# Last softmax blocks of two steps, weights divided first, products in PSUM, and step 0's weights straight from the gathered rows

## The chip, the cores and the metric

The kernel runs on one core of a Trainium2 chip. The metric is the device time of one execution in microseconds (us), as the median of repeated executions. One full pass is about 2.08 ms. The profiles are of single executions.

SBUF and PSUM are the two memories beside the engines (matmuls write to PSUM, which is handed out in banks), HBM is the large one outside. In profile lines PE is TensorE and PEld its weight loads, DVE is VectorE, ACT ScalarE, POOL GpSimd, and SP SyncE, which issues transfers (DMA). L952 is line 952 of that run's kernel, x8 a count of instructions, and the clock is the share of TensorE's full clock that was granted.

Two kinds of chip come up in this study. In three sets of runs the kernel before takes 2081 to 2082 us; in one set, all on one chip, it takes 2095.6 us (median of 45 runs). I call that kind of chip slow, and never compare a time of one kind with a time of the other. (This is my word: the record puts all timed runs but one in the fast state, and that one is unknown.) Points of profiles are compared across the two kinds in places; the chip column of the table below shows where.

## The reference

A recommender with a history of T = 100 steps, 128 features, 1024 samples. Cut to what matters:

```python
# phase 1: a GRU over the history, and an attention score for each of its states
_, gru_seq = scan(gru_step, h0, swapaxes(item_historical_embedding, 0, 1))
keys  = swapaxes(gru_seq, 0, 1)                       # (sample, step, feature)
score = mlp(concat([keys, q, keys - q, q * keys]), relu)
attn  = softmax(where(mask == 1, score, -inf), axis=1)
pooled = einsum('bt,btd->bd', attn, keys)
att_seq = pooled.T[:T]                                # feature t of pooled is step t's weight
# phase 2: a second recurrence (AUGRU), whose update gate is scaled by that weight
def augru_step(h, (x_t, a_t)):
    r = sigmoid(concat([h, x_t]) @ Wr.T + br)
    u = sigmoid(concat([h, x_t]) @ Wu.T + bu)
    h_hat = tanh(concat([h * r, x_t]) @ Wh.T + bh)
    u = a_t[:, None] * u
    return (1 - u) * h + u * h_hat
```

Phase 2 needs the *finished* pooled vector before its first step, so between the two loops there is a serial passage: finish the softmax, finish the pooling, bring the pooled rows into the order of phase 2 (sorted by length), start.

## The kernel before

The samples are in two halves of 512. The softmax is an online one in blocks of steps. Pooling is a multiplication of keys and weights and an addition; GpSimd does it during the loop, and after the loop GpSimd takes half 0 and VectorE takes half 1. The pooled rows are written to HBM, gathered in sorted order by indirect DMA, transposed on TensorE into a table of weights (one row for each step), written to HBM once more, and read back broadcast over the partitions, one row for a step. The parts that the change touches, cut (`...` marks cuts):

```python
ENDS = (*range(8, 89, 8), 92, 96, T)          # ends of the softmax blocks

def pool(self, count, eng):                   # VectorE or GpSimd
    ...
    w = e[:, self.ks, n].unsqueeze(2).to_broadcast(acc.shape)
    ...
    d = wp.tile([P, KH, R], F32, tag=tag, name="kw")      # SBUF
    eng.tensor_mul(d, k, w)
    eng.tensor_add(acc, acc, d)

# the end of phase 1
    ...
    for half in reversed(halves):             # mask * 1/den, then the last pooling
        nc.vector.tensor_mul(att[half.i], used, 1/den)
    for half, eng in zip(reversed(halves), (nc.vector, nc.gpsimd)):
        half.pool(T, eng)
        nc.vector.tensor_mul(att[half.i], att[half.i], pooled[:, half.ks, :])
        for p in range(P // R):
            nc.sync.dma_start(out=to[p], in_=att[half.i][p * R : (p + 1) * R])

# phase 2
def sort_weights(i, r, gates):                # r: the gathered rows of half i
    p = bank("pw") if i else pa.tile(...)
    for g in range(GH):
        nc.tensor.transpose(p[:, ts(g, P)], r[:, g, :], ident)
    rows_t = wp.tile([P, HB], F32, name="att_t", bufs=2)
    nc.vector.tensor_copy(rows_t, p)
    nc.sync.dma_start(out=att_d[i], in_=rows_t[:T, :])
    first = pa.tile([P, HB], F32, tag="a", name="first")
    nc.tensor.matmul(first, lhsT=ident[:, 0:1].to_broadcast([P, P]), rhs=rows_t, ...)
    u, h = gates
    nc.vector.tensor_mul(first, first, u)
    nc.vector.tensor_mul(h3[i], first, h)     # the state after step 0
    for t in (1, 2):
        load_att(t, i)                        # read the table's row t, broadcast
```

The pool `pa` has a single PSUM bank; `bank()` rotates through the other seven. The order of phase 2's start on TensorE, which is program order, is: gates of step 0, then the six input products of the gates of step 1 (`open_gates`), `sort_weights(0)`, the recurrent products of step 1 for half 0, `sort_weights(1)`, the transposes of the keys of step 2, the candidate product of step 1 (`ph<-r,wh`), and so on through the loop.

## Time and profile before

| kernel before | |
|---|---|
| time, median of 3 (range) | 2082.06 us (2079.63 to 2083.44) |
| span of the profiled execution | 2094.8 us |
| TensorE / VectorE busy | 97% / 84% |
| last GRU operation of phase 1 starts | 1414.67 us |
| first write of pooled rows to HBM | 1456.9 us |
| first recurrent product of phase 2 | 1474.6 us |

The page, the table by stretch and the waits are quoted in the prediction. One more view is needed for what follows: TensorE's own timeline where phase 2 starts. Each line has the start, the busy time of the group, engine, line, operation, output and inputs, shape, count, and in brackets how long the engine stood idle before it and what ended that.

```profile
1460.54 2.08 PE L967 MATMUL pr<-k,wr 128*128 128x512 f32 x2 [7.89 <-ACT k L954]
...
1469.74 0.33 PE L919 MATMUL pw<-ident,att_r 128*128 128x128 f32 x1 [0.98 <-DMA att_r<-pooled_d,idx]
...
1481.92 0.66 PE L953 MATMUL pk<-ident,rows 128*128 128x128 f32 x4 [1.52 <-DVE first L932]
1482.41 1.02 PE L971 MATMUL ph<-r,wh 128*128 128x512 f32 x2
```

TensorE has opened the gates of step 1 (from 1460.54 on) and then waits for the last gathered row of half 0, which lands at 1469.7. The last line, the candidate product of step 1, is the point from which the loop runs; call it the **restart**. The key transposes and the gates of step 0 were done long before, from 1441.3 to 1452.7, while VectorE still pooled.

### The profile page before, as it was taken

Reading aid. Unit: us, or ns where it says so; the run is one execution under the profiler, and the core shown is the slowest. Engines: PE = TensorE matmul, PEld = TensorE weight load, DVE = VectorE, ACT = ScalarE, POOL = GpSimd, SP = SyncE. Lnnn points to the kernel's source line nnn. Section 1 sums busy time; section 2 is a strip of 40 time slices with the busy share of each in tenths; the row PEclk is TensorE's granted clock in tenths of the full one; section 3 lists DMA queues with packets and bytes.
Section 4 is the critical chain, followed back from the end, with each engine's and each line's share of the span. In section 5 each row is a group of like instructions: output and inputs, shape, how many; then the busy total and the mean of one; then the engine's idle time right before and its main releaser. Section 6 shows DMA issues by size and latency. Waiting matters only on the chain. (4 is left out here: it accounts for less than half of the span.)

```text
span 2094.8 us, 26717 instructions
## 1 busy us (share of the span) xinstructions
PE 2042.1 (97%) x8292; PEld 977.6 (47%) x8292; DVE 1758.4 (84%) x3025; ACT 826.1 (39%) x1508; POOL 1302.3 (62%) x1301
## 2 busy tenths in 40 slices
PE   8999999999999999999999999996799999999998
PEld 3343333333333333333333333333344556678887
DVE  6888999999989988989898888998467777888786
ACT  3334343433434343433343333432343444445454
POOL 0234939579796959595969586796645444444332
PEclk9999999999999999999999999998999999999999
DMA  4643233333234434333433332222533333333331
GB/s 119 113 93 102 87 102 110 98 105 87 85 95 111 115 104 114 110 109 95 137 107 98 91 95 79 82 87 69 158 95 111 96 93 96 98 99 96 78 73 34
DMA packets 254611, 205.60 MB, mean 98 GB/s; under 512 B 75846, under 2 KB 216874, under 8 KB 254458
## 3 DMA queue, kind: packets, MB, share of 16 engines
q1 hardware_dynamic: 242138, 171.36, 29.5%
q0 software_dynamic: 12320, 32.44, 5.6%
q8 instruction: 67, 1.10, 0.2%
q14 instruction: 86, 0.70, 0.1%
HBM read 147.68 MB, written 54.40 MB: 96 GB/s over the span
## 5 line engine op out<-in xcount | busy, mean ns | idle before, releaser
L490 PE MATMUL ps<-x,wih 128*128 128x512 f32 x1200 | 592.7, 603 | 4.1 <-DMA x<-in_hist_x 4.1
L490 PE MATMUL ps<-hn,whh 128*128 128x512 f32 x1188 | 574.4, 592 | 0.0
L490 PEld LDWEIGHTS ps<-x,wih 128*128 128x128 f32 x1200 | 220.9, 190 | 327.7 <-issue 254.4
L490 PEld LDWEIGHTS ps<-hn,whh 128*128 128x128 f32 x1188 | 225.7, 190 | 284.1 <-issue 276.3
L476 POOL TENSOR_TENSOR xm<-x,m 128x512 f32<-128x512 f32 x200 | 246.5, 1233 | 127.3 <-DMA m<-mask_d 127.0
L521 ACT ACTIVATE ps<-ps,bih 128x512 f32<-128x512 f32 x200 | 132.4, 662 | 470.3 <-DVE ps L520 470.3
L502 ACT ACTIVATE r<-ps,brz 128x512 f32<-128x512 f32 x200 | 137.4, 687 | 394.4 <-PE ps L490 393.6
L477 POOL TENSOR_TENSOR hist<-hist,xm 128x512 f32<-128x512 f32 x200 | 265.8, 1329 | 15.7
L580 POOL TENSOR_TENSOR pooled<-pooled,kw 128x512 f32<-128x512 f32 x190 | 255.4, 1344 | 14.9
L579 POOL TENSOR_TENSOR kw<-kt,e 128x512 f32<-128x512 f32 x190 | 219.8, 1157 | 64.1 <-DVE e L735 64.0
L159 POOL DMA_INDIRECT rows<-keys_d,idx_k x208 | 202.2, 972 | 84.0 <-POOL rows L158 49.8
L559 DVE TENSOR_TENSOR kq<-hn,item 128x512 f32<-128x512 f32 x200 | 228.0, 1179 | 0.0
L638 PE MATMUL pm<-hn,wk 128*32 128x512 f32 x1200 | 213.3, 598 | 5.3 <-DVE f L672 3.6
L638 PE MATMUL pm<-kq,wkq 128*32 128x512 f32 x1200 | 210.9, 594 | 0.0
L979 ACT ACTIVATE c<-ph,bh 128x96 f32<-128x96 f32 (+42 forms) x198 | 96.7, 488 | 270.9 <-PE ph L971 228.2
L638 PE MATMUL pm<-mv,w 128*32 128x512 f32 (+1 forms) x808 | 198.2, 602 | 2.2 <-ACT mv L677 1.7
L995 DVE TENSOR_TENSOR pu<-pu,c 128x96 f32<-128x96 f32 (+42 forms) x197 | 88.8, 451 | 112.3 <-ACT c L979 90.6
L158 POOL COPY rows<-rest 128x1 f32<-128x1 f32 x208 | 39.1, 188 | 223.0 <-DVE rest L1005 218.7
L672 DVE TENSOR_TENSOR f<-pm,q 128x512 f32<-128x512 f32 x200 | 128.4, 684 | 55.8 <-PE pm L638 55.8
L525 DVE TENSOR_TENSOR d<-hn,ps 128x512 f32<-128x512 f32 x198 | 136.1, 687 | 34.9 <-ACT ps L521 32.6
L526 DVE TENSOR_TENSOR d<-ps,d 128x512 f32<-128x512 f32 x200 | 138.4, 692 | 23.8 <-ACT ps L522 7.1
L520 DVE TENSOR_TENSOR ps<-ps,u 128x512 f32<-128x512 f32 x200 | 140.0, 700 | 21.6 <-PE ps L490 0.5
(158 smaller groups left out, 3019.7 us busy)
## 6 DMA issues: line engine op xcount, KB each, us to landing
x<-in_hist_x SPq DMA_DIRECT2D x212, 256.0 KB
keys_d<-kt SPq DMA_DIRECT2D x46, 1024.0 KB
m<-mask_d SPq DMA_DIRECT2D x200, 128.0 KB
keys_d<-kt SPq DMA_DIRECT2D x64, 64.0 KB
rows<-keys_d,idx_k POOLq DMA_INDIRECT x208
s_b<-mv SPq DMA_DIRECT2D x200, 8.0 KB
mask_i<-in_mask SPq DMA_DIRECT2D x8, 200.0 KB
at<-att_d SPq DMA_DIRECT2D x32, 48.0 KB
```

Of the source, the lines that this page charges most:

```text
L159: nc.gpsimd.indirect_dma_start(out=r[:, k, :], out_offset=None, in_=keys_d[q], in_offset=bass.IndirectOffsetOnAxis(ap=idx_k[:, k, i : i + ...
L476: nc.gpsimd.tensor_mul(d, x, m)
L477: nc.gpsimd.tensor_add(acc, acc, d)
L490: nc.tensor.matmul(p, lhsT=w[:, g, :], rhs=v, start=(j == 0), stop=(j == len(parts) - 1),)
L502: nc.scalar.activation(r, pr, AF.Sigmoid, bias=brz[:, 0:1])
L520: nc.vector.tensor_add(pi, pi, u)
L525: nc.vector.tensor_sub(d, h, pi)
L526: nc.vector.tensor_mul(d, pz, d)
L559: nc.vector.tensor_mul(kq, h, item[:, self.cols])
L579: eng.tensor_mul(d, k, w)
L580: eng.tensor_add(acc, acc, d)
L638: nc.tensor.matmul(p[i][s, :], lhsT=w[:, s], rhs=v, start=start, stop=stop)
```

## The change

The intent is to shorten the passage. (a) The last block of four steps becomes two of two, so that GpSimd and VectorE can pool the first pair while the second is still being scored. (b) The weights are divided by their sum before pooling, so the two 512-column products of mask and reciprocal go. (c) The weights, and the products that VectorE makes in the tail, lie in PSUM, so that its operations don't read two operands from SBUF while GpSimd reads there too. (d) Half 1's last score rectification goes from VectorE to ScalarE. (e) Step 0's weights are taken from the gathered rows by four small broadcast matmuls, ahead of the transposes and the copy. (f) Converted keys get a pool of their own. For (c) six PSUM banks are set aside until the last pooling (`banks` below), and the products of the features (`pf`), which fill TensorE meanwhile, go to two of them in a changed order. The diff is cut (`...`), and long lines are shortened:

```diff
-ENDS = (*range(8, 89, 8), 92, 96, T)
+ENDS = (*range(8, 89, 8), 92, 96, 98, T)
@@ pool
+                    psum = eng is nc.vector and e[1] is not None
+                    w = e[psum][:, self.ks, n].unsqueeze(2).to_broadcast(acc.shape)
...
+                        if psum:
+                            d = blocked(banks["kw"])
+                        else:
+                            d = wp.tile([P, KH, R], F32, tag="kw", name="kw")
@@ scores
-                elif half.i:
-                    nc.vector.tensor_scalar(to, of, bias, 0.0, ALU.add, ALU.max)
@@ sums of the last block
                     nc.vector.reciprocal(den, den)
+                    nc.vector.tensor_mul(e[:, :, :rows], e[:, :, :rows], den ...)
+                if both[1] is not None:
+                    nc.vector.tensor_copy(both[0][:, :, :rows], e[:, :, :rows])
@@ end of phase 1
+        names = [ps.tile([P, HB], F32, tag="g", name="last") for _ in range(6)]
+        banks.update(e=names[:2], kw=names[2], pt=names[3], f=names[4:])
... (stages, pooling of block A by both engines, then of block B)
-        for half in reversed(halves):
-            nc.vector.tensor_mul(att[half.i], used, 1/den)
+        for half in halves:
+            nc.vector.tensor_mul(t, later["used"][:, half.ks, :], pooled[:, half.ks, :])
@@ sort_weights
+            first = pa.tile([P, HB], F32, tag="a", name="first")
+            for g in range(GH):
+                nc.tensor.matmul(first[:, ts(g, P)],
+                    lhsT=r[:, g, 0:1].to_broadcast([P, P]), rhs=ident, ...)
+            u, h = gates
+            nc.vector.tensor_mul(first, first, u)
+            nc.vector.tensor_mul(h3[i], first, h)
+            p = pa.tile([P, HB], F32, tag="a", name="pw") if i else bank("pw")
             ... transposes, copy, write of the table (as before)
-            first = ... (broadcast matmul from rows_t, the two products)
@@ load_key
-            k = wp.tile([P, HB], F32, name="k3", bufs=4)
+            k = qp.tile([P, HB], F32, name="k3")
```

More of the change, by code (lines that the diff above doesn't have):

```diff
@@ L568, in pool @@
                     acc = pooled[:, self.ks, :]
-                    w = e[:, self.ks, n].unsqueeze(2).to_broadcast(acc.shape)
+                    psum = eng is nc.vector and e[1] is not None
+                    w = e[psum][:, self.ks, n].unsqueeze(2).to_broadcast(acc.shape)
                     if t is None:
@@ L576, in pool @@
                     else:
-                        tag = "d" if eng is nc.vector else "kw"
-                        d = wp.tile([P, KH, R], F32, tag=tag, name="kw")
+                        if psum:
+                            d = blocked(banks["kw"])
+                        else:
+                            d = wp.tile([P, KH, R], F32, tag="kw", name="kw")
                         eng.tensor_mul(d, k, w)
@@ L607, in features @@
                 )
-                p = ps.tile([P, M0], F32, tag="g", name="pf")
+                p = banks["f"][g % 2][:, :M0]
                 for c, v in enumerate(comb):
@@ L624, in features, with blocked @@
                 yield
+        def blocked(t):
+            return t.rearrange("p (k r) -> p k r", r=R)
         halves = [Half(i) for i in range(NH)]
         left = {}
+        banks = {}
         def attend(t):
@@ L706, in softmax @@
             e = sp.tile([P, NK, 2 * G + 1], F32, name="e", bufs=3)
+            both = e, None
+            if banks:
+                b = banks["e"].pop()
+                both = e, b[:, : NK * (G + 1)].rearrange("p (k n) -> p k n", n=G + 1)
+                e = both[1]
+                top_n, den_n = (b[:, NK * m : NK * (m + 1)] for m in range(G + 1, G + 3))
             top = sp.tile([P, NK], F32, name="top", bufs=3)
             den = sp.tile([P, NK], F32, name="den", bufs=3)
-            soft.update(j=j + 1, top=top, den=den)
+            if both[1] is None:
+                top_n, den_n = top, den
+            soft.update(j=j + 1, top=top, den=den, e=both)
             def scores(i):
                 ks = ts(i, KH)
-                pt = pa.tile([P, KH, R], F32, tag="a", name="pt")
+                if banks:
+                    pt = blocked(banks["pt"])
+                else:
+                    pt = pa.tile([P, KH, R], F32, tag="a", name="pt")
                 nc.vector.transpose(
@@ L721, in tops @@
                 scores(1)
-                nc.vector.tensor_reduce(top, e[:, :, :n], AX.X, ALU.max)
+                nc.vector.tensor_reduce(top_n, e[:, :, :n], AX.X, ALU.max)
                 if j:
-                    nc.vector.tensor_max(top, top, top_old)
-                    nc.vector.tensor_sub(e[:, :, n], top_old, top)
+                    nc.vector.tensor_max(top, top_n, top_old)
+                    nc.vector.tensor_sub(e[:, :, n], top_old, top_n)
+                    if both[1] is not None:
+                        nc.vector.tensor_scalar_min(e[:, :, n], e[:, :, n], 0.0)
                 nc.vector.tensor_sub(
@@ L735, in sums @@
                 nc.vector.tensor_mul(e[:, :, :n], e[:, :, :n], on)
-                nc.vector.tensor_reduce(den, e[:, :, :n], AX.X, ALU.add)
+                nc.vector.tensor_reduce(den_n, e[:, :, :n], AX.X, ALU.add)
                 if j:
@@ L739, in sums @@
                     nc.vector.tensor_mul(old, den_old, e[:, :, n])
-                    nc.vector.tensor_add(den, den, old)
+                    nc.vector.tensor_add(den, den_n, old)
                 if last:
                     nc.vector.reciprocal(den, den)
+                    nc.vector.tensor_mul(
+                        e[:, :, :rows],
+                        e[:, :, :rows],
+                        den.unsqueeze(2).to_broadcast([P, NK, rows]),
+                    )
+                if both[1] is not None:
+                    nc.vector.tensor_copy(both[0][:, :, :rows], e[:, :, :rows])
                 for half in halves:
                     if j:
-                        half.todo.append((e, n, None))
-                    half.todo += [(e, t - b0, t) for t in range(b0, b1)]
+                        half.todo.append((both, n, None))
+                    half.todo += [(both, t - b0, t) for t in range(b0, b1)]
             soft["stages"] += [lambda: scores(0), tops, sums]
@@ L839, in gru_phase @@
         stage()
+        e, _ = soft["e"]
+        copy = banks["e"][0][:, : NK * (G + 1)].rearrange("p (k n) -> p k n", n=G + 1)
+        nc.vector.tensor_copy(copy, e[:, :, : G + 1])
+        for half in halves:
+            half.todo = [((w[0], copy if w[0] is e else None), n, t) for w, n, t in half.todo]
         halves[0].pool(T, nc.gpsimd)
@@ L847, in gru_phase @@
         some(features[1:2])
-        halves[1].pool(1, nc.vector)
+        halves[1].pool(2, nc.vector)
+        stage()
         take(T)
@@ L851, in gru_phase @@
         attend(T + 1)
-        some(features[2:6])
-        halves[1].pool(1, nc.vector)
+        some(features[2:4])
+        stage()
         take(T + 1)
+        exponents()
+        some(features[2:4])
         halves[1].pool(T, nc.vector)
-        some(features[2:6])
+        some(features[4:6])
+        stage()
+        halves[0].pool(T, nc.gpsimd)
         stage(2)
-        some(features[6:])
+        some(features[4:6])
         exponents()
         some(features[6:])
+        some(features[6:])
         stage()
-        att = [
-            t.rearrange("p (k r) -> p k r", r=R)
-            for t in s_bs[NH * (soft["j"] % 2) : NH * (soft["j"] % 2) + NH]
-        ]
-        for half in reversed(halves):
-            nc.vector.tensor_mul(
-                att[half.i],
-                later["used"][:, half.ks, :],
-                soft["den"][:, half.ks].unsqueeze(2).to_broadcast([P, KH, R]),
-            )
-        for half, eng in zip(reversed(halves), (nc.vector, nc.gpsimd)):
-            half.pool(T, eng)
-            nc.vector.tensor_mul(att[half.i], att[half.i], pooled[:, half.ks, :])
+        halves[0].pool(T, nc.gpsimd)
+        halves[1].pool(T, nc.vector)
+        for half in halves:
+            t = blocked(s_bs[NH * (soft["j"] % 2) + half.i])
+            nc.vector.tensor_mul(t, later["used"][:, half.ks, :], pooled[:, half.ks, :])
             to = pooled_d[half.cols, :].rearrange("(k r) (p c) -> p r k c", r=R, c=R)
             for p in range(P // R):
-                nc.sync.dma_start(out=to[p], in_=att[half.i][p * R : (p + 1) * R])
+                nc.sync.dma_start(out=to[p], in_=t[p * R : (p + 1) * R])
     def augru_phase(pools, widths, alive):
         wp = pools.enter_context(tc.tile_pool(name="wp3", bufs=3))
+        qp = pools.enter_context(tc.tile_pool(name="qp3", bufs=4))
         sp = pools.enter_context(tc.tile_pool(name="sp3", bufs=2))
@@ L914, in sort_weights @@
         def sort_weights(i, r, gates):
-            p = bank("pw") if i else pa.tile([P, HB], F32, tag="a", name="pw")
+            first = pa.tile([P, HB], F32, tag="a", name="first")
+            for g in range(GH):
+                nc.tensor.matmul(
+                    first[:, ts(g, P)],
+                    lhsT=r[:, g, 0:1].to_broadcast([P, P]),
+                    rhs=ident,
+                    start=True,
+                    stop=True,
+                )
+            u, h = gates
+            nc.vector.tensor_mul(first, first, u)
+            nc.vector.tensor_mul(h3[i], first, h)
+            p = pa.tile([P, HB], F32, tag="a", name="pw") if i else bank("pw")
             for g in range(GH):
@@ L922, in sort_weights @@
             nc.sync.dma_start(out=att_d[i], in_=rows_t[:T, :])
-            first = pa.tile([P, HB], F32, tag="a", name="first")
-            nc.tensor.matmul(
-                first,
-                lhsT=ident[:, 0:1].to_broadcast([P, P]),
-                rhs=rows_t,
-                start=True,
-                stop=True,
-            )
-            u, h = gates
-            nc.vector.tensor_mul(first, first, u)
-            nc.vector.tensor_mul(h3[i], first, h)
             for t in (1, 2):
```

## The prediction

> **What bounds the kernel now.** I read the page first, then stretches of the trace in a table of engine busy time, then the instructions in order of time of the passage between the two phases, then who waited for whom in that passage. The page says that TensorE carries the kernel:
>
> ```profile
> PE 2042.1 (97%) x8292; PEld 977.6 (47%) x8292; DVE 1758.4 (84%) x3025; ACT 826.1 (39%) x1508; POOL 1302.3 (62%) x1301
> ...
> PE   8999999999999999999999999996799999999998
> ```
>
> The second row is TensorE's busy share in 40 slices of 52 us. It is full but for one dip, the "67" near slice 28. None of the changed code runs in the two loops' steady parts, so the dip is what it can act on. The table by stretch (columns: length, then PE, PE load, DVE, ACT, POOL busy us with counts, granted clock, DMA share, GB/s) cuts the dip up:
>
> ```profile
> 1421.00:1434.00 13.00, 10.99 (x48) 5.34 (x43) 12.71 (x14) 3.16 (x6) 12.69 (x10) 1.00 0.57 165
> 1434.00:1443.00 9.00, 7.97 (x49) 7.42 (x47) 8.20 (x18) 2.19 (x7) 3.02 (x4) 1.00 0.22 79
> 1443.00:1457.00 14.00, 6.27 (x16) 2.94 (x16) 13.83 (x13) 1.78 (x3) 9.71 (x7) 0.88 0.03 10
> 1457.00:1470.00 13.00, 7.90 (x16) 3.40 (x16) 0.48 (x1) 3.96 (x7) 5.12 (x6) 0.74 0.32 61
> 1475.00:1493.00 18.00, 11.12 (x30) 4.65 (x29) 5.30 (x8) 3.82 (x7) 11.01 (x15) 0.93 0.79 254
> ```
>
> From 1421 to 1457 VectorE is full (34.7 of 36 us): it is the bound while the last softmax block and the last pooling steps are done. From 1457 to 1470 it is idle, and a chain of transfers holds: pooled rows are written to HBM, gathered in sorted order, transposed. The waits of 1420 to 1500 name both links:
>
> ```profile
> DVE att_t L921 <- PE pw L919: 12.6, 1, 12.6
> POOL att_r L135 <- DMA pooled_d<-s_b: 10.4, 1, 10.4
> ACT c L979 <- remote: 4.4, 1, 4.4
> ```
>
> The second loop's first recurrent matmul (L971) starts at 1474.59, and TensorE is steadily full only from about 1494. So the passage is a serial chain of some 70 us, and each us off it is a us off the end, up to where a parallel chain takes over.
>
> **What the Trainium skill says.** "SBUF — State Buffer", section "Who interferes with whom": a VectorE instruction with two SBUF inputs contends with a GpSimd instruction that reads SBUF, and one with at most one SBUF input does not. The trace agrees. These are VectorE's pooling steps of half 1, while GpSimd pools half 0 until about 1453, and after:
>
> ```profile
> 1450.25 1.56 DVE L579 TENSOR_TENSOR kw<-kt,e 128x512 f32<-128x512 f32 x1
> 1451.84 1.65 DVE L580 TENSOR_TENSOR pooled<-pooled,kw 128x512 f32<-128x512 f32 x1
> 1453.42 0.68 DVE L579 TENSOR_TENSOR kw<-kt,e 128x512 f32<-128x512 f32 x1
> 1454.13 0.69 DVE L580 TENSOR_TENSOR pooled<-pooled,kw 128x512 f32<-128x512 f32 x1
> ```
>
> Operations with a PSUM operand stay short all through, under a GpSimd that is 62% busy; two SBUF inputs average 1.18 us (page, groups):
>
> ```profile
> L559 DVE TENSOR_TENSOR kq<-hn,item 128x512 f32<-128x512 f32 x200 | 228.0, 1179 | 0.0
> L525 DVE TENSOR_TENSOR d<-hn,ps 128x512 f32<-128x512 f32 x198 | 136.1, 687 | 34.9 <-ACT ps L521 32.6
> ```
>
> "VectorE: DVE Perf Modes", section on the trn2 errata, gives PSUM sources a larger fixed cost than SBUF ones (120 against 58 cycles, 0.06 us). Here 687 ns against 680 to 690 ns uncontended says that it hardly shows at 512 elements; it may on the small softmax operations. "TensorE: Matmul & The Clock Gate", Part 1: idle windows of about 3.4 us halve TensorE's clock. The trace agrees: the clock column falls to 0.74 from 1457 to 1470, and the 512-column matmuls there start about 0.85 us apart instead of 0.43.
>
> **The change part by part.** (a) The final block of 4 steps becomes two of 2 steps; each block costs a chain of small operations. Before, transposes to subtraction took 1436.62 to 1439.46 (2.84 us), exponential and handover 0.4, the sums and reciprocal 1439.88 to 1442.57 (2.7, of which some 1.4 is two 32-column products stretched to 0.77 and 0.97 us by GpSimd). New: chain A about 3.1 us (one more operation, the clamp), A's sums 1.3 (five at about 0.25), chain B 3.1, exponential 0.45, B's sums with division and copy about 2.0.
>
> (b) Dividing the weights removes the two products of mask and reciprocal (L869, 2.90 us); one 96-column multiply of 0.3 us takes their place.
>
> (c) Weights and products in PSUM: each VectorE pooling operation falls from 1.4 to 1.75 us to about 0.72 start to start, since each now waits for the one before. GpSimd in turn falls from 1.52/1.60 to its free 1.07/1.27.
>
> (d) Half 1's last rectifications move from VectorE (0.76 us each) to ScalarE, which has room.
>
> Now the new schedule, from the built order and these durations. The sums of block 92 to 96 end at 1422.6 as before; a copy of its weights to PSUM costs 0.3, so all up to the rectifications slips 0.3. First five pooling operations: 1425.4 to 1428.9. Then VectorE must wait for the broadcast of step 97's scores: those small transfers stand behind two 1 MB writes of keys on the same queue (the issue at 1425.7 was held 3.5 us, and ScalarE's wait for its landing ended at 1432.7). So chain A runs from 1433.0 to 1436.1, four pooling operations to 1439.0, A's sums to 1440.3, B to 1443.4, exponential and sums to 1445.9, ten pooling operations (7.2) to 1453.1. GpSimd: block A's two steps from 1440.3 (1.1 + 2 x 2.34 = 5.8) to 1446.1, B's to 1451.9, just ahead. Mask product 0.7: the first write to HBM goes out at 1453.8, against 1456.90. **Gain 3.1 us.** About 4 us of VectorE's saving is lost idle before chain A, and some 4 more to the second block's chain.
>
> (e) Step 0's weights from gathered rows. Writes, landing and gathers keep their length (6.46 us from first issue to first gather, 6.3 to the last landing of half 0). Before: last transpose 1469.74, copy 1470.11, broadcast matmul from 1470.85 at half clock, product 1473.04, so 3.3 us. After: a 128-column matmul per gather, about 0.35 us after the last landing. **Gain 2.9 us** for half 0, so L971's matmul comes about 6 us earlier, near 1468.5. The transposes and the copy now follow the two products, so half 0's weight table goes to HBM 1.3 us later after its gather; but it landed by 1476.9 for a use at 1481.8, so there is slack. Half 1's copy was issued at 1479.25; by the same steps it comes at about 1474.8, **4.5 us earlier**, and its products 8 us earlier.
>
> What restarts the steady loop? Its first use of half 1's table needs write, read back and landing: the write of 1479.25 was answered only at 1483.19, the read landed about 1488, because 2 MB of gathered keys fill the queues (DMA share 0.79). Those gathers move by only 3.1 us. So not 6 to 8 but 3.5 to 6 us should reach the end. I take 5.5: 2082.06 - 5.5 = 2076.5. (f) The separate pool for the converted keys has as many buffers as before; it moves addresses and old waits only, 0.
>
> **The rivals.** First, *transfers hide it*: the read of the weight table for half 1 and the gathers set the restart, so that the removed copy and matmul are hidden and only 3.1 us remain: 2079. For it: the DMA share of 0.79 and 254 GB/s; against: half 1's write is issued 4.5 us earlier.
>
> Second, *the extra block eats the gain*: VectorE gets about 15 more small operations, and if each dependent PSUM operation costs 0.1 us more than I put (the errata's sign), and scores land later than 1433, chain A and B grow by 2 to 3 us: 2079 to 2082. Against: the mean of 687 ns.
>
> Third, *more is won*: the "remote" wait of ScalarE (4.35 us) and TensorE's hole of 3.6 us before 1489.65 are unexplained. The profiled execution took 2096.73 us where timed ones took 2082, so some of this may be the profiler's and not be there to win. If it is a real collision with the gathers that an earlier start avoids, 10 to 12 us come: 2070.
>
> **Range and chances.** The rivals span 2070 to 2082, and runs of before spread over 4 us. I give 2070 to 2081. For 2% the change would need 42 us, more than half of the whole passage, and no part of it could lose that much: within 2% has 0.98, either side 0.01.
>
> **What would show it.** In the changed profile: pooling operations of VectorE near 0.7 us while GpSimd works; an idle of some 4 us on VectorE before the first transpose of scores, ended by the DMA of the scores; the first write of pooled rows about 3 us earlier relative to the last GRU matmul; no 512-column broadcast matmul between last gather and product, with the recurrent matmul about 6 us earlier; half 1's weight table issued 4 to 5 us earlier. The busy row must show the same dip, somewhat narrower, and both loops unchanged. Wrong would be: a pooling operation on PSUM still above 1 us; GpSimd ending after VectorE, which would make it the bound of the phase's end; ScalarE's start of the second phase (its activation table and first gates) ending after the gathers; or a time outside 2070 to 2081.

## The result, and the profile after

The changed kernel is correct. It took 2074.07 us (median of 6, 2072.45 to 2076.12) where the kernel before, timed beside it, took 2081.99: ratio 0.9963, 95% interval 0.995 to 0.9976. Two later sets on two chips of the fast kind gave 0.9969 and 0.9970 (2075.09 and 2074.38 us against 2081.08 and 2081.02). A ratio is the mean time of one kernel's fast runs over that of the other's in the same rounds, so not quite the ratio of the medians. The gain is thus 6.2 to 7.7 us (0.0030 to 0.0037 of 2081.5), within 2%.

The page of the changed kernel, first execution, busy row and TensorE's slices:

```profile
PE 2035.2 (98%) x8304; PEld 981.2 (47%) x8304; DVE 1749.7 (84%) x3040; ACT 827.7 (40%) x1511; POOL 1299.1 (63%) x1302
...
PE   8999999999999999999999999997999999999998
```

The dip is one slice narrower ("7" in place of "67"). The same stretches as in the prediction's table (length, then busy us and count of PE, PE load, DVE, ACT and POOL, clock, DMA share, GB/s):

```profile
1421.00:1434.00 13.00, 11.57 (x57) 6.38 (x49) 8.85 (x15) 4.31 (x8) 10.61 (x10) 1.00 0.56 165
1443.00:1457.00 14.00, 5.94 (x16) 3.31 (x15) 9.09 (x17) 3.00 (x5) 7.78 (x7) 0.66 0.30 67
1457.00:1470.00 13.00, 11.40 (x41) 6.05 (x40) 1.99 (x3) 3.69 (x7) 8.91 (x10) 0.97 0.17 45
1475.00:1493.00 18.00, 18.00 (x47) 8.16 (x46) 10.93 (x17) 7.79 (x12) 12.41 (x21) 0.91 0.81 256
```

VectorE is no longer full before 1457 (8.85 of 13 us and 9.09 of 14 us), and in the last stretch TensorE is busy for all of the 18 us where it was for 11.12. The waits of 1420 to 1500 (engine, line, releaser: total, times, longest):

```profile
DVE first L960 <- PE first L952: 14.7, 2, 14.4
...
PE pk L987 <- DVE pooled L583: 8.1, 1, 8.1
...
POOL att_r L135 <- DMA pooled_d<-s_b: 7.2, 1, 7.2
DVE pu L1036 <- DMA at<-att_d: 7.2, 2, 3.7
```

The wait of GpSimd for the written rows is there as before, now 7.2 us. The second and the fourth line are new: TensorE waits for VectorE's last pooling, and VectorE waits twice for the weight table that comes back from HBM. VectorE's timeline of the changed kernel:

```profile
1432.39 0.73 DVE L732 STREAM_TRANSPOSE last<-s_b 128x512 f32<-128x512 f32 x1 [3.94 <-DMA s_b<-mv]
...
1446.36 0.69 DVE L582 TENSOR_TENSOR last<-kt,last 128x512 f32<-128x512 f32 x1
1447.09 0.69 DVE L583 TENSOR_TENSOR pooled<-pooled,last 128x512 f32<-128x512 f32 x1
```

Pooling operations last 0.69 us while GpSimd pools beside them, and the idle time of some 4 us before the first transposes of scores is there. TensorE's timeline at the start of phase 2:

```profile
1451.53 1.94 PE L987 MATMUL pk<-ident,rows 128*128 128x128 f32 x8 [8.06 <-DVE pooled L583]
...
1465.75 1.05 PE L952 MATMUL first<-ident,att_r 128*128 128x128 f32 x8
1466.64 0.60 PE L964 MATMUL pw<-ident,att_r 128*128 128x128 f32 x4
1468.46 1.13 PE L1005 MATMUL pr<-h,wr 128*128 128x512 f32 x2 [1.22 <-DVE h L961]
...
1472.94 0.63 PE L964 MATMUL pw<-ident,att_r 128*128 128x128 f32 x4 [1.61 <-DVE h L961]
1474.36 0.66 PE L987 MATMUL pk<-ident,rows 128*128 128x128 f32 x4 [0.79 <-DVE att_t L966]
1474.85 1.88 PE L1005 MATMUL ph<-r,wh 128*128 128x512 f32 x2
```

The broadcast matmuls `first` start at 1465.75 with no idle time before them: the gathered rows were not what they waited for. TensorE had just ended the gate products of step 1. Its opening of phase 2 had begun only at 1451.5, when VectorE's last pooling had freed the PSUM banks. The gathered row that came last for half 0 had landed at 1464.66 (the landings are in the trace). From 1474.85 on it does not stop again for more than 0.2 us before the end of the loop, near 2060; but its clock is 0.5 from 1474.9 to 1478.3.

To compare kernels I use times from the start of the last GRU operation of phase 1 (the same work lies before it in all): the first write of pooled rows, the first recurrent product, the restart (`ph<-r,wh` of step 1), and VectorE's operation `r<-h,pr` of the 13th half-step of phase 2, which lies in the steady loop. All in us, read from the timelines; the last column is the median of all timed runs, the others are of the profiled execution alone.

| kernel | chip | first write | first recurrent | restart | 13th half-step | median time |
|---|---|---|---|---|---|---|
| before, first profile | slow by its traits (below), chip not on record | 42.2 | 59.9 | 67.7 | 136.0 | 2082.06, timed on a fast one |
| before, again | slow | 42.2 | 58.9 | 67.6 | 138.9 | 2095.62 |
| changed, three sets | fast | 37.5 to 37.7 | 53.6 to 54.1 | 60.4 to 60.5 | 124.5 to 125.1 | 2074.07 to 2075.09 |
| changed, old order in `sort_weights` | slow | 37.7 | 55.0 | 62.9 | 133.1 | 2092.88 |
| changed, pooling in SBUF | slow | 42.5 | 57.4 | 71.1 | 136.2 | 2097.54 |
| changed, one last block | slow | 38.1 | 53.4 | 66.1 | 131.4 | 2092.64 |
| before with (e) alone | fast | 42.2 | 57.1 | 65.7 | 130.7 | 2079.66 |
| early key gathers | fast | 37.7 | 56.2 | 64.1 | 127.1 | 2078.79 |
| step 1 direct too | fast | 37.5 | 53.0 | 61.7 | 126.7 | 2076.99 |
| both of these | fast | 37.6 | 55.9 | 67.7 | 133.6 | 2080.22 |
| bank and ScalarE copy | fast | 37.7 | 53.8 | 58.9 | 123.4 | 2073.23 |
| these and a warm TensorE | fast | 37.5 | 53.5 | 59.0 | 122.2 | 2072.20 |

**The first profile of the kernel before is of the slow kind.** From the 13th half-step to the end it takes 544.1 us, the four kernels profiled on the slow chip take 543.2 to 544.2, and all nine profiles from fast chips take 532.2 to 532.7. So the 22.7 us between the spans of the first two profiles (2094.8 and 2072.1) are not the change; about 11.5 of them lie in the later loop, which the change does not touch. The five slow profiles share a second trait: they hold 15,390 to 15,594 records of landed transfers, the fast ones 17,777 to 17,811; and from 1462 to 1505 each of them has waits of 2.8 us and more whose releaser the profile cannot name ("remote" or "issue"), where no fast profile has one over 1.9 us. Such a wait is not in itself a stall: with fewer landing records, more releasers go unnamed. The first profile's chip is not on record, so that it is slow is an inference from these traits.

### The profile page after: what moved, and what is told of

It is laid out like the page before. It is cut to its first block, busy times and chain, and to the rows that moved or that the text cites. A ratio compares the mean times of both kernels' runs of the same rounds, so it can differ in the third digit from the quotient of the medians.

```text
span 2072.1 us, 26766 instructions
## 1 busy us (share of the span) xinstructions
PE 2035.2 (98%) x8304; PEld 981.2 (47%) x8304; DVE 1749.7 (84%) x3040; ACT 827.7 (40%) x1511; POOL 1299.1 (63%) x1302
## 5 line engine op out<-in xcount | busy, mean ns | idle before, releaser
L476 POOL TENSOR_TENSOR xm<-x,m 128x512 f32<-128x512 f32 x200 | 246.5, 1232 | 127.5 <-DMA m<-mask_d 127.1
L582 POOL TENSOR_TENSOR kw<-kt,e 128x512 f32<-128x512 f32 x190 | 217.6, 1145 | 64.1 <-DVE e L755 64.0
```

The source lines that it names most:

```text
L476: nc.gpsimd.tensor_mul(d, x, m)
```

## The experiments

All kernels below gave correct results. Twelve ran, in three sets of four; kernels of one set ran on one chip. Line numbers are those of each kernel and shift by a few.

### 1. The kernel before, again

No edit; it ran to see whether the hole in TensorE and the unexplained wait of ScalarE were an accident of one execution.

> The kernel before, profiled a second time. Its first profile took 2094.8 us where its six timed runs took 2079.6 to 2083.4; against the changed kernel's profile it loses 11.2 us by the 7th half step of the second loop and 11.6 us more after its 108th. Theory A (those later losses and the odd wait of ScalarE before 1489 are accidents of one execution, mine): the new profile's span is 2079 to 2084, the second loop's late half steps keep a constant distance to the changed kernel's, of some 8 us. Theory B (they are part of the kernel before and the change removes them): the span is again near 2095 and the distance again grows late in the loop.

This set landed on the slow chip: before took 2095.62 us there in 45 timed runs (2091.41 to 2098.58). This run took 2100.55 (one run, its state unknown). From the waits of 1462 to 1505:

```profile
ACT c L979 <- issue: 4.3, 1, 4.3
...
ACT pr L991 <- remote: 3.6, 1, 3.6
```

The stall came again, on another instruction too, with no releaser named. So it is no accident of one execution. The three other profiles of this set have such waits as well, and none of the nine fast profiles has: it belongs to the chip, not to the kernel before. Theory B's long span thus came, but not for its reason. What causes the stall on that chip stays open.

### 2. The changed kernel with the old order in `sort_weights`: (e) undone

```diff
 def sort_weights(i, r, gates):
-    four broadcast matmuls, two products; then transposes, copy, write
+    transposes, copy, write; then one 512-column broadcast matmul, two products
```

> The changed kernel with step 0's weights again by transpose, copy and broadcast matmul. Theory A (the prediction's: the copy and matmul lie on the path, 2.9 us for half 0): about 2 to 3 us slower than the changed kernel, 2076 to 2077.5. Theory B (the trip of the weight table through HBM ends the chain: VectorE waited 3.70 and 3.47 us for the loaded weights of step 1 in the changed kernel): half 0's table goes out about 1.3 us earlier here, half 1's about as late as before, so the restart moves by less than 1 us either way: 2073 to 2075. In the profile: the first recurrent matmul 2.9 us later in both theories, the first product with the loaded weights of half 0 later (A) or not (B).

2092.88 us (21 runs), ratio to before 0.9988 (0.9981 to 0.9994) on the slow chip. The first write is at 37.7, the restart at 62.9: 4.8 us ahead of before (67.7 and 67.6) and 2.4 us behind the changed kernel (60.5). So (a) to (d) bring the restart 4.8 us forward by themselves, and (e) 2.4 us more, the latter read across the two kinds of chip. The first recurrent product comes 0.9 to 1.3 us later than in the changed kernel, not the 2.9 of both theories. Theory A's 2 to 3 us fits the restart; in time it can't be checked, since the changed kernel was never timed on this chip. Of the 4.8, only 2.5 us (0.0012 of 2095.6) are in the time. The 13th half-step comes 70.2 us after the restart here and 64 to 65 in the changed kernel, with waits of 5.3 us (VectorE) and 3.6 us (ScalarE) between that have no named releaser; but before loses as much there on this chip (68.3 and 71.2), so where the other 2.3 us went is not shown.

### 3. The changed kernel with VectorE's pooling back in SBUF: (c) undone

```diff
-                    psum = eng is nc.vector and e[1] is not None
+                    psum = False
...
-                            d = wp.tile([P, KH, R], F32, tag="kw", name="kw")
+                            d = wp.tile(..., tag="d" if eng is nc.vector else "kw", ...)
```

> The changed kernel with VectorE's pooling weights and products in SBUF again; blocks of two steps, division first and softmax in PSUM stay. Prediction's step (c): pooling operations go back from 0.69 us to 1.4 to 1.75 us while GpSimd pools, so the ten last ones cost some 5 to 8 us more, GpSimd's 1.07/1.27 us go back to 1.5/1.6; the first write of pooled rows comes 5 to 7 us later and the time is 2079 to 2081, most of the gain gone. Rival (the order of stages and the division made the gain, PSUM did not): within 1 us of the changed kernel.

2097.54 us (21 runs), ratio 1.0012 (1.0005 to 1.0018): slower than before by 2.5 us. (The softmax's small operations stay in PSUM here; only the pooling goes back.) VectorE's timeline of this kernel, at the steps that took 0.69 us in PSUM:

```profile
1448.72 1.75 DVE L582 TENSOR_TENSOR kw<-kt,e 128x512 f32<-128x512 f32 x1
1450.50 1.45 DVE L583 TENSOR_TENSOR pooled<-pooled,kw 128x512 f32<-128x512 f32 x1
```

The first write comes at 42.5, no earlier than in the kernel before (42.2). That is 4.8 to 5.0 us later than in the changed kernel, where 5 to 7 were expected. So without its pooling in PSUM nothing is left of the gain at the first write: the rival, that order and division made it, is out. The restart (71.1) has stalls of over 5 and 2 us before it in this profile, so only the first write is to be read here, and the 2.5 us may hold some of the chip.

### 4. One last block of four steps: (a) undone

```diff
-ENDS = (*range(8, 89, 8), 92, 96, 98, T)
+ENDS = (*range(8, 89, 8), 92, 96, T)
```

with the tail's stages put back in one chain.

> The changed kernel with one last block of four steps (96 to 100) instead of two of two, the rest kept. Theory A (the block of two pays: GpSimd can start earlier): VectorE is done earlier (one chain of 4.4 us less, but its scores land only at about 1436.2, so its last pooling operation ends near 1447 to 1448 instead of 1451.2), GpSimd starts its four last steps only near 1441 and needs 1.1 + 4 x 2.34 = 10.5 us, so it ends near 1451.5 and the first write of pooled rows is within 1 us of the changed kernel's: 2073 to 2076. Theory B (the second block's chain is pure loss, rival two of the prediction): 2 to 4 us faster, 2070 to 2072.

2092.64 us (9 runs), ratio 0.9984 (0.9974 to 0.9994). The first write comes at 38.1, 0.4 to 0.6 us later than with two blocks, as Theory A has it; Theory B's earlier write did not come. VectorE is done with half 1 at 1449.2 and then waits for GpSimd's half 0:

```profile
1453.68 1.29 DVE L903 TENSOR_TENSOR s_b<-used,pooled 128x512 f32<-128x512 uint8 x2 [4.47 <-POOL pooled L583]
```

GpSimd can't start the last four steps until the single block is summed, and needs 10.5 us for them. Two blocks let it start earlier, but give VectorE a second chain; the difference is 0.4 to 0.6 us. The restart lies at 66.1, but two stalls of over 3 us without a named releaser stand before it in this profile, so only the first write is to be read here.

### 5. The changed kernel again, beside three variants

> The changed kernel as it is, as the standard for the runs beside it, and to compare with the three variants of the first set. On the first chip it was 0.9963 of before. If that ratio holds on this chip, some 2088 us where before takes 2095 (about 2074 where before takes 2082), and then undoing the direct weights of step 0 (0.9988) costs 5 us, undoing the PSUM pooling (1.0012) costs 10 us, and one last block instead of two (0.9984) costs 4 us. Rival: the gain depends on the chip, and here the ratio is near 0.9985; then the two last blocks and the direct weights would be worth next to nothing on their own. In the profile: the wait of VectorE for the broadcast weight table of step 1 (3.7 and 3.5 us in the first profile of the changed kernel) should be there again if it is a property of the schedule and not an accident.

2075.09 us against 2081.08: ratio 0.9969 (0.9957 to 0.9981). The chip was of the fast kind, so how the changed kernel does on the slow chip was not measured, and the ratios of runs 2 to 4 can't be set beside this one as times. The waits for the table were there again (3.7 and 3.4 us), so they belong to the schedule.

### 6. Key gathers ahead of the row gathers

```diff
+        ahead1 = gathers(1)
+        for _ in range(5):
+            next(ahead1)
         sorted_rows = [gather_weights(i) for i in range(NH)]
...
-        all_of(gathers(1))
+        all_of(ahead1)
```

> Five of the eight gathers of key rows for steps 4 to 7 (1.3 MB of 2 MB) are issued ahead of the gathers of the sorted weight rows; three stay after them. Theory: the weight table's way through HBM (write answered after 3.4 us for half 0, 6.3 us for half 1, then the read-back) is slowed by the 2 MB of row gathers issued at the same time. Then here the answers come after about 2 to 3.5 us, the two waits of VectorE for the table shrink from 3.7 and 3.5 us to 1 to 2 each, and the time falls by 2 to 4 us under the changed kernel. Rival: the length of a small write and read-back is fixed whatever else runs; then the waits stay at 3.5 us and the time stays within 1 us.

2078.79 us (21 runs), ratio 0.9985 (0.9979 to 0.9992): 3.7 us *slower* than the changed kernel. The waits of VectorE for the table did shrink, to 0.52 and 1.65 us. The table's way (from the issue of its write to the product that reads it) got shorter, 7.3 and 6.1 us against 8.9 and 10.3 in run 5, as the theory said; but VectorE also came to it later. GpSimd's timeline shows what the transfers collided with instead:

```profile
1458.09 0.95 POOL L135 DMA_INDIRECT rows<-keys_d,idx  x1 [0.30 <-issue]
1462.58 0.95 POOL L135 DMA_INDIRECT att_r<-pooled_d,idx  x1 [3.53 <-DMA pooled_d<-s_b]
```

The five gathers were issued while the writes of the pooled rows were under way, and GpSimd could gather these 3.5 us later (47.7 us after the last GRU operation in place of 44.2). The restart moved from 60.4 to 64.1 and the 13th half-step from 124.5 to 127.1. The profiled execution was the fastest of the 21 (2076.39 against 2073.86 of run 5's profile). The time followed this chain, not the waits for the table.

### 7. Step 1's weights straight from the rows as well

```diff
-            for t in (1, 2):
-                load_att(t, i)
+            load_att(2, i)
...
+            if t == 1:
+                weights_of_rows(1, i)    # four broadcast matmuls, ScalarE's copy to SBUF
```

> The weights of step 1 as well are taken straight from the gathered rows, by four broadcast matmuls and a copy by ScalarE into SBUF; only steps from 2 on use the table in HBM. Theory: in the changed kernel the end of the chain into the steady second loop is the table's way through HBM (VectorE waits 3.70 and 3.47 us for it at step 1), which I had put down as slack. Then those two waits go, the later read for step 2 becomes the next limit (it lands some 5 us after that of step 1 is needed), and the time falls by 3 to 7 us. Rival: ScalarE and TensorE set the restart (a clock that is still halved, gates queued behind key copies), so the waits of VectorE are beside the path; then the time stays within 1 us, or rises by 1 us for the eight extra matmuls.

2076.99 us (11 runs), ratio 0.9978 (0.9969 to 0.9987): 1.9 us slower than the changed kernel. Both waits for the table are gone; yet the theory's 3 to 7 us did not come. TensorE's timeline:

```profile
1475.14 1.11 PE L1000 MATMUL pk<-ident,rows 128*128 128x128 f32 x4 [0.78 <-DVE att_t L966]
...
1479.81 1.05 PE L973 MATMUL row<-ident,att_r 128*128 128x128 f32 x8
```

TensorE runs without a pause from 1475.14 on, as it does without this edit, and now has the eight extra matmuls (some 0.9 us for each half) in its way; those of half 0 also hold the single bank for half 1's `first`. So VectorE's waits for the table lay beside the path.

### 8. Both edits

> Both: early gathers, and step 1's weights straight from the rows. If the table's way is the limit and both act on it, the gains do not add up: as fast as the better of the two, perhaps 1 us beyond, since the read for step 2 then lands earlier. If each acts on another link they add (up to 8 us). If neither is on the path all four runs agree within 1 us.

2080.22 us (21 runs), ratio 0.9995 (0.9989 to 1.0002): 5.1 us slower than the changed kernel, so the two losses (3.7 and 1.9 us) nearly add up. The restart is at 67.7. None of the three answers that I had written down came.

### 9. The changed kernel, third time

> The changed kernel once more, as the standard on the chip of this set: 0.9963 and 0.9969 of before on two occasions so far. If this set runs on a chip where before takes 2095 us, as the first set did, and the ratio is 0.996 to 0.997 there too, then the first set's ratios (0.9988 without the direct weights, 0.9984 with one last block, 1.0012 without PSUM) may be set beside it as they are. If the ratio is near 0.9985 there, the changed kernel gains less on a slow chip and those differences shrink.

2074.38 us against 2081.02: ratio 0.9970 (0.9959 to 0.9982), again a fast chip.

### 10. The kernel before with (e) alone

The same edit as run 2, applied to the kernel before in the other direction.

> Before, with nothing but the direct weights of step 0. In the kernel before, TensorE had opened the gates of step 1 at 1467.5 us and then waited for the gathered rows, so here the removal acts fully: the first recurrent matmul should come 2.5 to 3.3 us earlier, half 1's products 4 us or more, and the time falls by 3 to 5 us (ratio 0.9976 to 0.9986). If the parts simply add, this and the first set's run without the direct weights (0.9988, 2.5 us) make up the whole change (6.4 to 7.9 us). Rival: the direct weights pay only behind the earlier first write, because of the collision with the gathers of key rows; then here the time falls by under 1.5 us.

2079.66 us (13 runs), ratio 0.9991 (0.9983 to 0.9999): 1.9 us, less than the 3 to 5 expected. Up to the gathers this kernel is the kernel before, and its profile is from a fast chip, so it stands in for before there. TensorE's timeline:

```profile
1469.71 0.49 PE L919 MATMUL first<-ident,att_r 128*128 128x128 f32 x2 [0.70 <-DMA att_r<-pooled_d,idx]
...
1477.69 1.06 PE L931 MATMUL pw<-ident,att_r 128*128 128x128 f32 x4 [1.61 <-DVE h L928]
1479.54 1.12 PE L954 MATMUL pk<-ident,rows 128*128 128x128 f32 x4 [0.79 <-DVE att_t L933]
```

Here `first` does wait for the gathered rows. The first recurrent product comes 1.8 to 2.8 us earlier than in the two profiles of before, and the restart 1.9 to 2.0 us earlier (65.7). From this kernel to the changed one, that is (a) to (d) on top of (e), the restart moves by 5.3 us and the time by 5.3 us (2079.66 to 2074.38). The sum that was asked for before the run, 1.9 us here and 2.5 in run 2, is 4.4 and not the 6.2 to 7.7 of the whole; but the 2.5 is from the slow chip. At the restart, 1.9 and 4.8 make 6.7 of some 7.2.

### 11. A bank of its own for half 1's transposes, and ScalarE's copy

```diff
-            p = pa.tile([P, HB], F32, tag="a", name="pw") if i else bank("pw")
+            p = bank("pw")
...
-            nc.vector.tensor_copy(rows_t, p)
+            nc.scalar.copy(rows_t, p)
```

> Half 1's transposed weights go to a PSUM bank of the gates instead of the one bank that holds step 0's weights, and ScalarE, which is idle then, copies the transposed weights to SBUF instead of VectorE. Theory: what restarts the second loop in the changed kernel is TensorE in its program order, which stands still 1.61 us for VectorE's product that frees the bank and 0.79 us for VectorE's copy before the key transposes; from 1474.4 us on it never waits, so that VectorE's waits for the table (3.7 and 3.5 us) cost nothing. Then here both holes go, the recurrent candidate matmul of step 1 comes 1.3 to 1.7 us earlier, the tables go out 1.2 and 1.7 us earlier, and the time falls by 1 to 2.5 us under the changed kernel. Rival: the table's way is the limit after all and takes over, then the gain is at most the 1.2 us of its earlier write; or nothing changes.

2073.23 us (5 runs), ratio to before 0.9962 (0.9948 to 0.9976), 1.15 us below the changed kernel's median of the same set; the two ranges (2072.00 to 2073.66 and 2072.98 to 2075.87) overlap. In the profile the restart comes 1.5 us earlier (58.9 against 60.4). TensorE's timeline:

```profile
1473.38 0.63 PE L987 MATMUL pk<-ident,rows 128*128 128x128 f32 x4 [1.17 <-DVE h L961]
...
1486.42 1.13 PE L1005 MATMUL ph<-r,wh 128*128 128x512 f32 x2 [1.24 <-DVE r L1031]
```

The two holes of 1.61 and 0.79 us have become one of 1.17. And TensorE's clock stays full after the restart, where all three profiles of the changed kernel have 0.5 for the next 3.4 us. But a new hole of 1.24 us stands at 1486.42: VectorE was late with `r`, because it had waited for half 1's table:

```profile
1483.74 0.70 DVE L1036 TENSOR_TENSOR pu<-pu,at 128x512 f32<-128x512 f32 x1 [4.75 <-DMA at<-att_d]
```

So the table's way through HBM, which cost nothing before this edit, is the next limit. After that hole TensorE is still 1.3 us ahead of run 9's profile (the third `ph<-r,wh` comes at 71.5 and 72.8 us after the last GRU operation). Theory and rival were each right in part.

### 12. The same, and TensorE kept warm

```diff
         halves[1].pool(T, nc.vector)
+        for _ in range(32):
+            nc.tensor.matmul(banks["f"][0][:, :P], lhsT=ident, rhs=ident, start=True, stop=True)
```

> The same, and 32 small matmuls of the identity, whose result nobody reads, in TensorE's idle time before the end of the first phase (8 us in which it waits for VectorE's last pooling to free the PSUM banks), so that its clock isn't halved when the second phase opens. Theory: the opening of the second phase on TensorE (from the last pooling to the sixth gate matmul, 13.7 us in the changed kernel, 5.8 us of them at half clock) and the writes and gathers of the pooled rows end within 0.5 us of each other. Then the opening ends some 2.5 us earlier here, TensorE then waits for the gathered rows, and the time falls by less than 1 us against the run before it. Rival: the opening alone is the limit, and 2 us or more are won. The other way: the extra matmuls delay something and the time rises.

2072.20 us (5 runs), ratio to before 0.9957 (0.9944 to 0.9971): 1.0 us below run 11 by the medians, and the lowest of all; with five runs of each and ranges that overlap, this 1.0 us is not clear of the noise. TensorE's timeline:

```profile
1451.95 1.06 PE L988 MATMUL pk<-ident,rows 128*128 128x128 f32 x8 [1.38 <-DVE pooled L583]
...
1464.83 0.49 PE L953 MATMUL first<-ident,att_r 128*128 128x128 f32 x2 [0.23 <-DMA att_r<-pooled_d,idx]
1466.09 0.49 PE L953 MATMUL first<-ident,att_r 128*128 128x128 f32 x2 [0.77 <-DMA att_r<-pooled_d,idx]
```

The granted clock from 1443 to 1457 is 1.00 where it is 0.66 without the edit (table by stretch). The eight key transposes take 1.06 us in place of 1.94, the gate products of step 1 end some 2 us earlier, and `first` then waits for the gathers: the opening of phase 2 on TensorE and the chain of writes and gathers do end close together, as the theory has it (though in this profile the gathers came 0.8 us later than in run 11, 45.0 against 44.2 us after the last GRU operation, for a reason not shown). The first recurrent product moves by only 0.4 us and the restart not at all; what differs later is that the hole of 1.24 us is gone. Half 1's table was written at the same time as in run 11 (58.0 and 57.9), yet VectorE could go on with it at 67.7 in place of 68.8:

```profile
1482.45 0.70 DVE L1037 TENSOR_TENSOR pu<-pu,at 128x512 f32<-128x512 f32 x1 [4.75 <-DMA at<-att_d]
```

Half 0's table went out 0.4 us earlier; whether that, or chance, brought half 1's back sooner is not shown. The versions of runs 11 and 12 are better than both kernels by their medians and by the steps in the profile; the ranges of run 12 (2070.54 to 2072.77) and of the changed kernel in the same set (2072.98 to 2075.87) do not overlap.

## Why the prediction was right, and where it was not

The total was 6.2 to 7.7 us where 5.5 was predicted, and the medians, 2074.07 to 2075.09, lie in the range. It came out so near in part by luck: one step gained about 1.5 us more than put and another 1.6 to 2 us less. By its own steps:

**Pooling in PSUM (c).** Right: 0.69 us, start to start 0.72, under a GpSimd at its free 1.07 and 1.27. Run 3 shows that this carries the gain of the first write.

**The idle time before the first block.** Right: 3.94 us, ended by the transfer of the scores.

**The first write, "Gain 3.1 us".** The mechanism was right and the size too small: 4.5 to 4.7 us (42.2 to 37.5 and 37.7). The small operations of the two chains were put 0.8 us too long together. The sums of the last block ended at 1444.4, not 1445.9; the ten pooling operations took 7.0, not 7.2; the first chain began 0.6 us ahead, 0.3 of it by the loop's earlier end. The rival that the extra block eats the gain was wrong in sign: 32-column operations in PSUM took 0.18 to 0.20 us. Still, run 4 shows that the second block by itself is worth just 0.4 to 0.6 us at the first write.

**The direct weights (e), "Gain 2.9 us for half 0".** This step failed, and the earlier write hid it in the sum ("about 6 us earlier" came out as 4.8 to 6.3). In the changed kernel `first` follows TensorE's gate products without a pause; the rows had landed. With the earlier write, a second chain that I had listed only among what would make me wrong, the opening of phase 2, became as long as the gathers and 0.4 to 1.1 us longer: it now starts when VectorE frees the PSUM banks (8.06 us of waiting), and 6 of its 14 us run at half clock. So on top of (a) to (d), (e) won 0.9 to 1.3 us for half 0 (run 2 against the changed kernel, across the two kinds of chip), not 2.9; in the kernel before it won 1.8 to 2.8. Run 12 takes the opening away, and the gathers are there right behind it.

**Half 1.** Right: from the first profile of before to that of the changed kernel its products came 8.8 us earlier (8 predicted), and its table was issued 4.6 us earlier (4.5).

**"Weight table of half 0 ... so there is slack."** Wrong by the waits: VectorE waited 3.70 us for it. But harmless, as run 7 shows.

**"What restarts the steady loop? Its first use of half 1's table."** Wrong. What restarts it is TensorE's program order. Half 1's `first`, its two products on VectorE, the freed bank, the transposes and the copy stand ahead of the key transposes in TensorE's queue. The Trainium skill says it in "PSUM — Partial Sum Buffer", section "Engine vs sequencer instructions": matmuls start and complete in program order. The trace agrees: half 0's `ph` had its input `r` at 1471.07 but started at 1474.85, behind half 1's `pw` and the key transposes `pk`, which waited 1.61 and 0.79 us. In the fast profiles the time goes with the restart, to within some 3 us: from the restart to the 13th half-step they take 63 to 66 us, and the profiled execution's own time less its 13th half-step is 1948.4 to 1949.6. I reasoned from the wrong limit to "3.5 to 6 us should reach the end"; the restart moved by 7.2 us in all, (a) to (d) 4.8 to 5.3 and (e) 1.9 to 2.4, and 6.2 to 7.7 us are in the time. (The restart of the kernel before is read from slow profiles, which is a weakness of that sum; from run 10 to the changed kernel, both on a fast chip, the restart and the time moved by the same 5.3 us.) The step that failed here is the limit: half 1's table was put as what restarts the loop, and the runs show TensorE's queue in its place. The term was 0.7 to 2.2 us too small, and the reason given for it was the wrong one.

**The third rival**, that the "remote" wait and the hole of 3.6 us might be there to win: no. They are in the five slow profiles and in none of the nine fast ones. I had read a profile of one kind of chip beside times from the other.

**Not tested alone:** (b), (d) and (f), the softmax's small operations in PSUM, and the new order and banks of the feature products. The changed kernel was not run on the slow chip, so runs 2 to 4 are set beside it by their profiles only.

## What to carry to other kernels

Where a passage between two phases is shortened, list every chain that enters its end, and on an engine with a program order put the engine's own queue on that list: here TensorE's order decided, and removing waits of VectorE that looked costly (7 us) gained nothing or lost time. Before a transfer is moved to relieve one wait, look at what it will overlap at its new place. And if a profile's span disagrees with the timed runs of the same kernel by more than their spread, compare a long untouched stretch first; it may be from another kind of chip.

## What the Trainium skill lacked or had wrong

- The Trainium skill, "VectorE: DVE Perf Modes", section on the trn2 errata: the larger fixed cost of PSUM sources made no visible difference here, 0.69 us against 0.68 to 0.69 us from SBUF for the same 512 columns; 32 columns took 0.18 to 0.20 us with a PSUM operand and 0.19 us from SBUF (before, `top<-top`).
- The Trainium skill, "DMA: Bandwidth & Descriptors", section "Anatomy of one DMA — SWDGE (gpsimd) path": a fixed cost of about 2 us. The gathers of pooled rows landed in 2.4 to 2.7 us. But a 200 KB table, which SyncE and not GpSimd writes, beside 2 MB of gathers let the read behind it go out only after 2.5 to 3.4 us (half 0) and 5.6 to 6.3 us (half 1) in the changed kernel, at 256 GB/s in all. How far the fixed cost grows for a small transfer among large ones is not said there.
- No page says which operations of GpSimd lose how much to the contention: its pooling operations take 1.07 and 1.27 us beside a VectorE that works in PSUM, and took 1.52 and 1.60 beside one that worked in SBUF (before).
- No page says that chips differ: 2081 to 2082 us against 2095.6 us for the same kernel, with 10.5 to 12 us of it after the 13th half-step of phase 2, and profiles of the slow kind lack 12 to 14% of the landing records (15,390 to 15,594 against 17,777 to 17,811).
